# One pair of resident B tiles instead of four rotating ones in a selective scan on one core

## The chip, the cores and the metric

The kernel runs on one core of one Trainium2 chip, as one program without collectives. The metric is the device time of one execution in microseconds (us), the median of several executions. All data is float32.

## The reference

Input is an image of 2 x 48 x 48 positions with 768 channels. Two layers follow each other, `x = x + layer(_gn(x))` for both, where `_gn` is a group normalization. The first is neighbourhood attention: 12 heads of 64, each position attends to a 7 x 7 window. The second is a bidirectional Mamba block, and it takes nearly all the time. For each image its 2304 positions are a sequence, and 1536 inner channels carry 16 states each. In one direction, the part that the change touches computes:

```python
def _selective_scan(u, delta, A, Bm, Cm):
    def step(h, inp):
        d_t, B_t, C_t, u_t = inp
        dA = jnp.exp(d_t[..., None] * A)
        h = dA * h + (d_t * u_t)[..., None] * B_t[:, None, :]
        y = jnp.einsum('bdn,bn->bd', h, C_t)
        return (h, y)
...
x_dbl = jnp.einsum('bdl,ed->bel', x, x_proj_w)
dt = x_dbl[:, :dt_rank]
Bm = x_dbl[:, dt_rank:dt_rank + n]
Cm = x_dbl[:, dt_rank + n:]
delta = jax.nn.softplus(jnp.einsum('brl,dr->bdl', dt, dt_proj_w) + dt_proj_b[None, :, None])
y = _selective_scan(x, delta, A, Bm, Cm) + x * Dp[None, :, None]
```

So the state of (channel, state number) is a first-order recurrence along the sequence. Its factor is exp(delta * A), its input is delta * u * B, and B and C depend on position and state number but not on channel. The second direction runs over the reversed sequence with weights of its own.

## The kernel before

**Tiling.** Channels lie on the 128 partitions, in ND = 12 tiles; the sequence runs along the free axis in NCH = 6 chunks of CL = 384 positions. A pass is one image (b) and one direction (back), and `passes` lists the 24 chunks in their order: image 0 forward, image 0 backward, image 1 forward, image 1 backward. One unit is one chunk and one channel tile k, so there are 288 units, 12 per chunk. The 16 states of a unit are worked in NSG = 4 groups of SG = 4.

**One group (`group` in `scan`).** A tile `hb` of four rows of 386 cells holds four states side by side, each with a spare cell ahead of and behind its 384 positions.

- L1231, ScalarE (ACT): copies eight numbers from `state`, or zeros in the first chunk of a pass, into the spare cells (columns 0 and 385) of the four rows of the B tile `bc[g]`. These are the states that enter the chunk, with a cell that restarts the recurrence at a row's end. The copy is made per unit, because each channel tile has its own states while the B values are the same for all twelve.
- L1225, VectorE (DVE) or GpSimd (POOL): the fill. It multiplies delta*u (in PSUM as `du` for DVE, in SBUF as `u` for POOL) by `bc[g]` into `hb`. It reads all 386 columns, so it needs both the load and the copy.
- L1247, ACT: one exponential per state, into one of the two PSUM tiles `da0` and `da1`, which hold two states each.
- L1258, DVE: one scan instruction for two states. It frees that `da` tile, so ACT can be two scans ahead at most.
- L1273, POOL: the product with C, from `bc[NSG + g]`. L1281, ACT: keeps the leaving states in `state`. L1290, TensorE (PE): transposes and sums the four states into `py`.

**The tiles of B and C.** For each chunk `chunk` takes eight new tiles with tags bc0 to bc7, one buffer per tag, and SyncE (SP) loads each with one broadcast from `xdf` or `xdb` (L1381, 768 KB): bc0 to bc3 are B with 386 columns, of which the load writes columns 1 to 384; bc4 to bc7 are C. A load waits until the last fill of the chunk before (unit k = 11) has read its tile.

**What sets the order.** `add` only lists a piece of work with its engine, an estimated duration and a key (a due time in units). What it reads and writes is given in buffers and numbered parts of them. `Order.run` plans all of it ahead: per engine it picks a work whose predecessors are done, EARLY work with a bonus of 20 units, and an order over all engines comes out. The instructions are then issued in that order, each engine runs its own in order, and the tile framework adds the semaphores for what it finds overlapping in memory. In the plan a load occupies SP for 400 ns and its data is there some 2.1 us plus its transfer later. In the plan of before, the first copy of a chunk (k = 0) depends on the load, since the load is listed as writing all parts of `bc[g]`, the ends (part 1) among them.

Attention of image 0 runs ahead of the scan phase and uses the same tags for other tiles: `FIRST` names them for `oT`, q and v, and `HEAD` for the first chunk's projections. Attention of image 1 and the projections run beside the scans, as jobs in the gaps.

Of the kernel before, what the change touches and what calls it, by code (L numbers as in the profile page):

```python
# [10 lines left out]
F32 = mybir.dt.float32  # L11
# [82 lines left out]
class Order:  # L94
# [15 lines left out]
    @staticmethod  # L110
    def cells(uses):
        for x in uses:
            buf, parts = x if isinstance(x, tuple) else (x, range(x.parts))
            for p in (parts,) if isinstance(parts, int) else parts:
                yield buf, p
# [130 lines left out]
def tile_kernel(  # L246
# [30 lines left out]
        Buf(f"da{i}", parts=2, ap=psum.tile([P, 1024], F32, tag=f"da{i}", name=f"da{i}"))  # L277
        for i in range(2)
    ]
    zero = res.tile([P, SG, 2], F32, tag="zero", name="zero")  # L280
    nc.gpsimd.memset(zero, 0.0)
    one = res.tile([P, KB, 2], F32, tag="one", name="one")
    nc.gpsimd.memset(one, 1.0)
# [35 lines left out]
    def sb(tag, shape, n, parts=1):  # L319
        return Buf(f"{tag}_{n}", wk, shape, tag, BUFS.get(tag, 1), parts)  # L320
# [8 lines left out]
    def add(eng, ns, fn, key, r=(), w=(), job=False, size=0, after=None, early=0, alt=None, due=False, opens=None):  # L329

        news = [x[0] if isinstance(x, tuple) else x for x in w]

        def issue():
            for v in news:
                if v.ap is None:
                    v.ap = v.pool.tile(v.shape, F32, tag=v.tag, name=v.name, bufs=v.bufs)
            fn()

        if eng == "PE":

            ns *= 1.04 if key < 0 else 1.05
        return order.add(eng, ns, issue, key, r, w, job, size, after, early, alt, due, opens)
# [837 lines left out]
    def scan(ch, k, x, dlj, duj, vt):  # L1180
# [30 lines left out]
        def group(g):  # L1211
            m = f"{n}_{g}"
            now = at + 0.25 * g
            hb = sb("hb", [P, SG * W], m, SG + 1)
            body = (hb, range(SG))
            kept = lambda o: state[:, k, 2 * SG * g + o : 2 * SG * (g + 1) + o].rearrange(
                "p (j e) -> p j e", e=2
            )
            was = zero if ch["first"] else kept(0) if back else kept(1)

            def first():
                by, on = (dus[:, ju, :], nc.gpsimd) if filled.eng == "POOL" else (du[:, :W], nc.vector)
                on.tensor_mul(  # L1225
                    cells(hb, SG), by.unsqueeze(1).to_broadcast([P, SG, W]), bc[g].ap
                )

            if k == 0 or not ch["first"]:
                add(  # L1230
                    "ACT", 98, lambda: nc.scalar.copy(bc[g][:, :, ends], was), now - 0.4,  # L1231
                    [(state, k * NSG + g)], [(bc[g], 1)], early=EARLY,
                )
            on = {"DVE": dve(SG * W), "POOL": SG * W * 2.03 + 15}
            main, other = ("DVE", "POOL") if g in (0, 1) else ("POOL", "DVE")
            filled = add(
                main, on[main], first, now - (0.35 if main == "POOL" else 0.1),
                [du, duj, bc[g]], [hb], after=marks.get(marks["n"] - 6),
                alt=(other, on[other]) if g in (1, 2, 3) else None,
            )  # L1240

            def step(j):
                i = g * SG + j
                da = das[j // 2 % 2]
                add(
                    "ACT", act(cl, 1) + 45,
                    lambda: nc.scalar.activation(  # L1247
                        cells(da, 2)[:, j % 2, h], dl[:, jd, c], AF.Exp, scale=q["A"][:, k, i : i + 1]
                    ),
                    now + 0.06 * j - 0.06, [dlj], [(da, j % 2)], due=True,  # L1250
                )

            def two_steps(j):
                da = das[j // 2 % 2]
                at2 = (slice(None), slice(j * W, (j + 2) * W))
                mark = add(
                    "DVE", (4 * W + 42) / 0.96,
                    lambda: nc.vector.tensor_tensor_scan(  # L1258
                        flip(hb[at2]), flip(da[:, : 2 * W]), flip(hb[at2]), 0.0, ALU.mult, ALU.add
                    ),  # L1260
                    now + 0.06 * j, [da], [(hb, (j, j + 1, SG))],
                )
                marks[marks["n"]] = mark
                marks["n"] += 1

            for j in range(0, SG, 2):
                step(j)
                step(j + 1)
                two_steps(j)

            add(
                "POOL", SG * cl * 2.03 + 10,
                lambda: nc.gpsimd.tensor_mul(  # L1273
                    cells(hb, SG)[:, :, h], cells(hb, SG)[:, :, h], bc[NSG + g][:, :, c]
                ),
                now + 0.25, [body, bc[NSG + g]], [body],
            )
            if not ch["final"]:
                add(
                    "ACT", 90,  # L1280
                    lambda: nc.scalar.copy(  # L1281
                        kept(0)[:, :, 1:2], cells(hb, SG)[:, :, leaves : leaves + 1]
                    ),
                    now + 0.3, [body, (hb, SG)], [(state, k * NSG + g)],
                )

            def add_up():
                for j in range(SG):
                    for t in range(nt):
                        nc.tensor.matmul(  # L1290
                            py[:tp, t * P : (t + 1) * P], cells(hb, SG)[:, j, h][:, tb[t]], ident,
                            start=False,
                            stop=g == NSG - 1 and j == SG - 1 and t == nt - 1,
                            is_transpose=True, skip_group_check=True,
                        )

            add(
                "PE", SG * nt * 109 + 60, add_up, now + 0.45, [body, py], [py], early=FIRM,
                opens=False if g == NSG - 1 else None,
            )  # L1300
# [62 lines left out]
    def chunk(b, back, i, at):  # L1363

        l0, cl = CHUNKS[i]
        s = f"{b}_{back}_{i}"
        dt = sb("dt", [RK + 1, CL], s)
        src = xd[back][b]
        add(
            "SP", 400, lambda: nc.sync.dma_start(dt[:, :cl], src[: RK + 1, l0 : l0 + cl]), at - 1.4,  # L1370
            [(src, cols(l0, cl))], [dt], size=RK * cl * 4,
        )
        bc = []
        for g in (0, 1, 2, NSG, 3, NSG + 1, NSG + 2, NSG + 3):

            o = int(g < NSG)
            t = sb(f"bc{g}", [P, SG, CL + 2 * o], s, 1 + o)
            r = RK + 1 + g * SG
            add(
                "SP", 400,  # L1380
                lambda t=t, r=r, o=o: nc.sync.dma_start(  # L1381
                    t[:, :, o : o + cl], src[r : r + SG, l0 : l0 + cl].partition_broadcast(P)
                ),
                at - 1 + 0.25 * (g % NSG) + 0.3 * (g >= NSG), [(src, cols(l0, cl))], [t],
                size=P * SG * cl * 4,
            )
            bc.append((g, t))
        bc = [t for g, t in sorted(bc, key=lambda x: x[0])]
        ends = (0, NCH - 1)

        ys = ()
        if (b, back, i) == passes[-1]:
            parts = [sb(tag, [P, n, CL], f"y{tag}{n}", n) for tag, n in (("uz", 2 * KB), ("uz", KB), ("u", KB))]
            ys = [(y, k) for y in parts for k in range(y.parts)]
        return dict(
            q=par[back], b=b, back=back, l0=l0, cl=cl, dt=dt, bc=bc, s=s, i=i, ys=ys,
            first=i == ends[back], final=i == ends[not back],
        )


    passes = [
# [4 lines left out]
    ]  # L1406

    FIRST = {
        "xn": ("xc", "uz"), "oT": ("bc0", "bc1", "bc2", "bc3"), "halves": 2, "k": ("hb",), "q": ("bc4", "bc5"),
        "v": ("bc6", "bc7"), "s": 0, "pt": 1, "po": ("py", "du"), "vw": ("u", "dlt"),  # L1410
        "ev": ("ev", "vt"),
    }
# [3 lines left out]
    }  # L1416
    LATE = 4
    FIRM = 4.0
    HEAD = ("bc4", "bc5", "bc6", "bc7", "bc0", "bc1")
    A0, A1, P1 = (-56, -16), (50, 118), 118  # L1420
    norms, norms0, stats = [], [], []
    for b in range(nb):
# [37 lines left out]
    for p, (b, back, i) in enumerate(passes):  # L1460
        ch = None
        for k in range(ND):
            units.append((p, b, back, i, k))
    chunks = {}

    deltas = {}

# [8 lines left out]
    for x, (p, b, back, i, k) in enumerate(units):  # L1476
        if x % KB == 0 and x + KB < len(units):
            ahead(x + KB)
        scan(chunks[p], k, x, *deltas.pop(x))
        if x == len(units) - 1:  # L1480
            ch = chunks[p]
            last_out_proj(b, ch["l0"], ch["cl"], ch["ys"], x - 1, x + 3)
        elif back and k == ND - 1:
            for h, (l0, cl) in enumerate(PIECES[i]):
                at = x + 2.5 + 5 * h if b else 188 + 2 * (2 * (NCH - 1 - i) + h)
                out_proj(b, l0, cl, at, at + (4.5 if b else 1.8))
# [55 lines left out]
```

## Time and profile before

| what | value |
|---|---|
| median of 3 runs | 7038.78 us (7036.31 to 7051.21) |
| span of the profiled execution | 7054.5 us |
| profiled execution's own time | not given apart from its span |
| DVE busy, 1060 to 7020 us | 5631.57 of 5960 us |
| POOL busy, same stretch | 5436.23 us |
| PE busy, same stretch | 5333.59 us |
| ACT busy, same stretch | 4654.78 us |
| scans (L1258) | 2304 of 1746 ns |
| fills (L1225) | 657 on DVE of 1743 ns, 495 on POOL of 3203 ns |
| products with C (L1273) | 1152 of 3186 ns |
| exponentials (L1247) | 4608 of 584 ns |
| copies of entering states (L1231) | 960 of 197 ns, and 16 of zeros |
| broadcast loads (L1381) | 192 of 768 KB |

The first 1036 us are attention of image 0 and projections; the scan phase fills the rest. A line number such as L1231 is that of the kernel before. The busy times are per engine; idle time matters only where the engine bounds the end. "[0.73 <-DMA bc<-xdb]" behind an instruction says that its engine stood idle for 0.73 us before it and that the last thing to come was that transfer. SPq is SyncE's queue of transfers: its rows show the issue and not the transfer's end.

### The profile page before, as it was taken

How to read it: one execution, taken by the hardware profiler on the slowest of the kernel's cores; microseconds unless marked ns; L12 is line 12 of the kernel's file. 1: busy time of each engine (PE TensorE's matmuls, PEld its weight loads, DVE VectorE, ACT ScalarE, POOL GpSimd, SP SyncE). 2: the span in 40 equal slices, each digit the busy share in tenths (PEclk: the TensorE clock that was granted, in tenths of full speed). 3: DMA queues.
4: the chain of work that ended last, by engine and by line, in shares of the span. 5: the costliest groups of instructions: out<-in, count | busy, mean ns of one | idle time of the engine just before them, and what ended most of it. 6: DMA issues, size and time to landing. Idle time of an engine off the chain costs nothing.

```text
span 7054.5 us, 105645 instructions
## 1 busy us (share of the span) xinstructions
PE 6334.5 (90%) x38151; PEld 4844.6 (69%) x38151; DVE 6061.2 (86%) x6217; ACT 4970.2 (70%) x10948; POOL 5447.5 (77%) x1951
## 2 busy tenths in 40 slices
PE   7999989999989998999988888888888898999888
PEld 5666656666667776676666656666678887777777
DVE  2354449999999999998898999999999999999998
ACT  1333248788887788887888778788876667777765
POOL 0000008888989999988898878999999999999997
PEclk9999989999999999999999999999999999999999
DMA  6565454444556444555444354343466676655553
GB/s 190 172 200 172 139 161 131 134 144 151 157 160 191 151 149 141 152 170 150 126 144 131 113 166 127 107 143 108 140 179 191 174 220 199 191 177 158 162 169 105
DMA packets 1337698, 1101.32 MB, mean 156 GB/s; under 512 B 136328, under 2 KB 1327416, under 8 KB 1337144
## 3 DMA queue, kind: packets, MB, share of 16 engines
q1 hardware_dynamic: 1337176, 1094.56, 52.1%
q8 instruction: 303, 4.96, 0.3%
q14 instruction: 219, 1.79, 0.1%
HBM read 881.41 MB, written 213.57 MB: 155 GB/s over the span
## 4 chain that ended last, share of the span: by engine, by line
DVE 39%; PE 19%; ACT 14%; POOL 12%; issue 9%; DMA 6%; SPq 1%; DVEq 0%; POOLq 0%; ACTq 0%
DVE hb L1258 25%; POOL hb L1273 8%; DVE hb L1225 7%; ACT da L1247 4%; PE mm_qk L382 4%; DVE uz_u L935 4%; POOL hb L1225 3%; PE py L1290 2%; PE mm_ao L382 2%; PE mm_v L382 2%; PE mm_xin L382 2%; ACT uz_u L928 1%; PE da L825 1%; ACT pr L785 1%; ACT L1163 1%
## 5 line engine op out<-in xcount | busy, mean ns | idle before, releaser
L1258 DVE TENSOR_TENSOR_SCAN hb<-da,hb 128x772 f32<-128x772 f32 x2304 | 3924.9, 1746 | 187.3 <-ACT da L1247 155.1
L1273 POOL TENSOR_TENSOR hb<-hb,bc 128x1536 f32<-128x1536 f32 x1152 | 3653.7, 3186 | 381.0 <-DVE hb L1258 338.3
L1247 ACT ACTIVATE da<-dlt,A 128x384 f32<-128x384 f32 x4608 | 2677.2, 584 | 915.2 <-DVE hb L1258 845.8
L1290 PE MATMUL py<-ident,hb 128*128 128x128 f32 x13824 | 1754.3, 279 | 264.3 <-POOL hb L1273 255.2
L1290 PEld LDWEIGHTS py<-ident,hb 128*128 128x128 f32 x13824 | 1570.9, 143 | 523.5 <-POOL hb L1273 413.6
L1225 POOL TENSOR_TENSOR hb<-u,bc 128x1544 f32<-128x1544 f32 x495 | 1584.6, 3203 | 22.6 <-PE py L1290 14.9
L1225 DVE TENSOR_TENSOR hb<-du,bc 128x1544 f32<-128x1544 f32 x657 | 1141.4, 1743 | 34.3 <-ACT du L1202 24.8
L1175 POOL TENSOR_TENSOR u<-dlt,u 128x384 f32<-128x384 f32 x288 | 263.8, 918 | 532.7 <-DMA bc<-xdf 412.6
L382 PE MATMUL mm_xin<-xc,w_x 128*128 128x390 f32 x1656 | 593.3, 504 | 25.3 <-DVE uz_u L935 16.2
L382 PE MATMUL mm_z<-xc,w_z 128*128 128x384 f32 x1728 | 608.1, 492 | 7.8 <-ACT dlt L1157 4.9
L382 PE MATMUL mm_out<-stage_y,w_o 128*128 128x192 f32 x3168 | 560.7, 332 | 18.1 <-ACT dlt L1157 6.4
L1491 PE MATMUL py<-ident 128*128 128x128 f32 x4431 | 550.4, 277 | 0.0
L382 PEld LDWEIGHTS mm_out<-stage_y,w_o 128*128 128x128 f32 x3168 | 522.0, 194 | 29.3 <-ACT dlt L1157 10.6
L1491 PEld LDWEIGHTS py<-ident 128*128 128x128 f32 x4431 | 503.3, 143 | 28.9 <-issue 26.0
L901 POOL MEMSET xc<- 128x18 f32 x4 | 0.5, 116 | 637.2 <-DVE sm L779 637.2
L382 PEld LDWEIGHTS mm_xin<-xc,w_x 128*128 128x128 f32 x1656 | 311.3, 195 | 238.3 <-issue 36.7
L935 DVE SCALAR_TENSOR_TENSOR uz_u<-mm_xin,conv_w,uz_u 128x384 f32<-128x384 f32 x792 | 428.3, 607 | 52.0 <-ACT uz_u L928 49.4
L382 PE MATMUL mm_qk<-xc_xn,w_qk 128*128 128x384 f32 x1296 | 459.1, 500 | 14.7 <-DMA w_qk<-in_w_qkv 3.1
L382 PEld LDWEIGHTS mm_z<-xc,w_z 128*128 128x128 f32 x1728 | 314.3, 192 | 194.4 <-issue 8.9
L382 PEld LDWEIGHTS mm_qk<-xc_xn,w_qk 128*128 128x128 f32 x1296 | 240.2, 194 | 173.8 <-issue 19.5
L785 ACT ACTIVATE pr<-pr,sm 128x308 f32<-128x308 f32 x432 | 234.5, 544 | 127.5 <-DVE sm L779 127.2
L1306 PE MATMUL py<-ident,vt 128*128 128x128 f32 x864 | 156.3, 292 | 146.3 <-ACT yt L1316 145.9
(163 smaller groups left out, 6780.9 us busy)
## 6 DMA issues: line engine op xcount, KB each, us to landing
w_o<-in_w_opT SPq DMA_DIRECT2D x264, 384.0 KB
bc<-xdf SPq DMA_DIRECT2D x96, 768.0 KB
bc<-xdb SPq DMA_DIRECT2D x96, 768.0 KB
w_qk<-in_w_qkv SPq DMA_DIRECT2D x144, 384.0 KB
w_x<-in_w_inT SPq DMA_DIRECT2D x144, 384.0 KB
w_z<-in_w_inT SPq DMA_DIRECT2D x144, 384.0 KB
w_ao<-in_w_out SPq DMA_DIRECT2D x72, 384.0 KB
u<-uf SPq DMA_DIRECT2D x48, 576.0 KB
```

Source lines behind the costliest of these rows:

```text
L382: nc.tensor.matmul(acc[:m, o0 : o0 + cl], wb[:, wi, wo : wo + m], xb[:, xi, xo : xo + cl], start=c == 0, stop=c == n - 1,)
L785: nc.scalar.activation(pr[j].ap, pr[j].ap, AF.Exp, bias=sm[:, j : j + 1], scale=-1.0, accum_out=sm[:, 2 + j : 3 + j],)
L825: nc.tensor.transpose(bank(pt, 512 - P)[:nk, k * P : (k + 1) * P], pr[j][:, c0 : c0 + nk], ident,)
L935: nc.vector.scalar_tensor_tensor(u, px[:, at[j] : at[j] + cl], q["conv_w"][:, k, j : j + 1], u, ALU.mult, ALU.add,)
L1175: lambda j=j: nc.gpsimd.tensor_mul(u[:, j, h], dl[:, j, c], u[:, j, h]), at + 0.06 + 0.25 * j,
L1225: on.tensor_mul(cells(hb, SG), by.unsqueeze(1).to_broadcast([P, SG, W]), bc[g].ap)
L1247: lambda: nc.scalar.activation(cells(da, 2)[:, j % 2, h], dl[:, jd, c], AF.Exp, scale=q["A"][:, k, i : i + 1]),
L1258: lambda: nc.vector.tensor_tensor_scan(flip(hb[at2]), flip(da[:, : 2 * W]), flip(hb[at2]), 0.0, ALU.mult, ALU.add),
L1273: lambda: nc.gpsimd.tensor_mul(cells(hb, SG)[:, :, h], cells(hb, SG)[:, :, h], bc[NSG + g][:, :, c]),
L1290: nc.tensor.matmul(py[:tp, t * P : (t + 1) * P], cells(hb, SG)[:, j, h][:, tb[t]], ident, start=False, stop=g == NSG - 1 and j == SG - 1 a ...
L1306: nc.tensor.matmul(py[:tp, t * P : (t + 1) * P], vt[:, tb[t]], ident, start=t == 0, stop=False, is_transpose=True, skip_group_check=True,)
L1491: nc.tensor.matmul(marks["py"][:, CL : CL + P], ident, ident, start=False, stop=False, is_transpose=True, skip_group_check=True,)
```

## The change

B's four tiles become two tiles `pairs` of eight states (tags bc0 and bc2, [128, 8, 386] each). They are taken once, when the scan phase begins, and kept to its end. Each has three parts in the planner's book: 0 and 1 are the two halves of four rows, 2 is the spare cells of all eight rows. The loads stay as they are in number, size and key, but each now lists only its half as written, and they are listed when the chunk's first unit is (`broadcasts`), no longer three units ahead. The copy of entering states is made once for two groups: 16 numbers in place of two times eight, with a planned 110 ns in place of 98, listed when the even group is. It reads the states of both groups, writes part 2, and lists the chunk's columns of `xdf` or `xdb` as read. The fill of a group reads its half and part 2. C's tiles stay. `FIRST` and `HEAD` follow: `oT` takes one tile of six channel pairs from bc0 or bc2 where it took two of three, and the last `HEAD` tile is bc2 where it was bc1.

```diff
-            was = zero if ch["first"] else kept(0) if back else kept(1)
+            pair, half = bc[g // 2], g % 2
...
-                    cells(hb, SG), by.unsqueeze(1).to_broadcast([P, SG, W]), bc[g].ap
+                    cells(hb, SG), by.unsqueeze(1).to_broadcast([P, SG, W]),
+                    pair[:, half * SG : (half + 1) * SG, :],
...
-            if k == 0 or not ch["first"]:
+            if half == 0 and (k == 0 or not ch["first"]):
+                was = zero if ch["first"] else kept(0 if back else 1, 2)
                 add(
-                    "ACT", 98, lambda: nc.scalar.copy(bc[g][:, :, ends], was), now - 0.4,
-                    [(state, k * NSG + g)], [(bc[g], 1)], early=EARLY,
+                    "ACT", 110, lambda: nc.scalar.copy(pair[:, :, ends], was), now - 0.4,
+                    [(state, k * NSG + g), (state, k * NSG + g + 1), (xd[back][b], cols(l0, cl))], [(pair, 2)], early=EARLY,
                 )
...
-                [du, duj, bc[g]], [hb], after=marks.get(marks["n"] - 6),
+                [du, duj, (pair, half), (pair, 2)], [hb], after=marks.get(marks["n"] - 6),
...
-        bc = []
-        for g in (0, 1, 2, NSG, 3, NSG + 1, NSG + 2, NSG + 3):
-
-            o = int(g < NSG)
-            t = sb(f"bc{g}", [P, SG, CL + 2 * o], s, 1 + o)
...
+    def broadcasts(ch, at):
+
+        src, l0, cl, s = xd[ch["back"]][ch["b"]], ch["l0"], ch["cl"], ch["s"]
+        if not pairs:
+            pairs.extend(
+                sb(f"bc{2 * p}", [P, 2 * SG, CL + 2], "pair", 3) for p in range(NSG // 2)
+            )
+        bc = []
+        for g in (0, 1, 2, NSG, 3, NSG + 1, NSG + 2, NSG + 3):
+
+            r = RK + 1 + g * SG
+            if g < NSG:
+                t, part, wide = pairs[g // 2], g % 2, slice(1, cl + 1)
+                of = slice(part * SG, (part + 1) * SG)
+                w = (t, part)
+            else:
+                t, of, wide = sb(f"bc{g}", [P, SG, CL], s), slice(0, SG), slice(0, cl)
+                bc.append(t)
+                w = t
+            add(
+                "SP", 400,
+                lambda t=t, r=r, of=of, wide=wide: nc.sync.dma_start(
+                    t[:, of, wide], src[r : r + SG, l0 : l0 + cl].partition_broadcast(P)
+                ),
+                at - 1 + 0.25 * (g % NSG) + 0.3 * (g >= NSG), [(src, cols(l0, cl))], [w],
+                size=P * SG * cl * 4,
+            )
+        ch["bc"] = pairs + bc
...
-        "xn": ("xc", "uz"), "oT": ("bc0", "bc1", "bc2", "bc3"), "halves": 2, "k": ("hb",), "q": ("bc4", "bc5"),
+        "xn": ("xc", "uz"), "oT": ("bc0", "bc2"), "halves": 1, "k": ("hb",), "q": ("bc4", "bc5"),
...
-    HEAD = ("bc4", "bc5", "bc6", "bc7", "bc0", "bc1")
+    HEAD = ("bc4", "bc5", "bc6", "bc7", "bc0", "bc2")
...
             ahead(x + KB)
+        if k == 0:
+            broadcasts(chunks[p], x)
         scan(chunks[p], k, x, *deltas.pop(x))
```

More of the change, by code (lines that the diff above doesn't have):

```diff
@@ L279, in tile_kernel @@
     ]
-    zero = res.tile([P, SG, 2], F32, tag="zero", name="zero")
+    zero = res.tile([P, 2 * SG, 2], F32, tag="zero", name="zero")
     nc.gpsimd.memset(zero, 0.0)
@@ L1215, in group @@
             body = (hb, range(SG))
-            kept = lambda o: state[:, k, 2 * SG * g + o : 2 * SG * (g + 1) + o].rearrange(
+            kept = lambda o, n=1: state[:, k, 2 * SG * g + o : 2 * SG * (g + n) + o].rearrange(
                 "p (j e) -> p j e", e=2
             )
-            was = zero if ch["first"] else kept(0) if back else kept(1)
+            pair, half = bc[g // 2], g % 2
             def first():
@@ L1273, in group @@
                 lambda: nc.gpsimd.tensor_mul(
-                    cells(hb, SG)[:, :, h], cells(hb, SG)[:, :, h], bc[NSG + g][:, :, c]
+                    cells(hb, SG)[:, :, h], cells(hb, SG)[:, :, h], bc[2 + g][:, :, c]
                 ),
-                now + 0.25, [body, bc[NSG + g]], [body],
+                now + 0.25, [body, bc[2 + g]], [body],
             )
@@ L1372, in chunk @@
         )
-        bc = []
-        for g in (0, 1, 2, NSG, 3, NSG + 1, NSG + 2, NSG + 3):
-            o = int(g < NSG)
-            t = sb(f"bc{g}", [P, SG, CL + 2 * o], s, 1 + o)
[L1378 to L1388, printed above, removed]
         ends = (0, NCH - 1)
@@ L1395, in chunk @@
         return dict(
-            q=par[back], b=b, back=back, l0=l0, cl=cl, dt=dt, bc=bc, s=s, i=i, ys=ys,
+            q=par[back], b=b, back=back, l0=l0, cl=cl, dt=dt, s=s, i=i, ys=ys,
             first=i == ends[back], final=i == ends[not back],
         )
+    def broadcasts(ch, at):
[24 more added lines that the diff above has]
+        ch["bc"] = pairs + bc
     passes = [
@@ L1463, in tile_kernel @@
             units.append((p, b, back, i, k))
-    chunks = {}
+    chunks, pairs = {}, []
     deltas = {}
```

## The prediction

> **What bounds the kernel now.** I read the busy time of each engine first, then the groups of instructions, then who waited for whom on ACT and DVE between 1060 and 7020 us, and last the order of time around one change of chunk.
>
> ```profile
> span 7054.5 us, 105645 instructions
> 1060.00:7020.00 5960.00, 5333.59 (x32999) 4186.83 (x32998) 5631.57 (x4701) 4654.78 (x10100) 5436.23 (x1936) 0.98 0.52 154
> ```
>
> The second line is the scan phase: PE 5334, its weight loads 4187, DVE 5632, ACT 4655, POOL 5436 us of 5960. DVE works 94% of the phase and sets its length; POOL, which takes the C products and 495 of the fills, is close behind with 91%. ACT has 1305 us idle, so making ACT's work shorter pays only where DVE waits for ACT.
>
> ```profile
> L1258 DVE TENSOR_TENSOR_SCAN hb<-da,hb 128x772 f32<-128x772 f32 x2304 | 3924.9, 1746 | 187.3 <-ACT da L1247 155.1
> L1231 ACT COPY bc<-state 128x8 f32<-128x8 f32 x960 | 182.9, 197 | 126.6 <-DVE hb L1225 64.6 <-POOL hb L1225 29.7 <-DMA bc<-xdb 15.1
> ACT da L1247 <- DVE hb L1258: 845.8, 1242, 3.8
> ACT bc L1231 <- DVE hb L1225: 64.6, 129, 4.1
> ACT bc L1231 <- POOL hb L1225: 29.7, 48, 1.6
> ACT bc L1231 <- DMA bc<-xdb: 16.6, 13, 3.3
> ACT bc L1231 <- DMA bc<-xdf: 12.8, 12, 2.4
> DVE uz_u L935 <- ACT uz_u L928: 37.6, 36, 3.9
> DVE hb L1225 <- ACT du L1202: 16.3, 22, 1.7
> ```
>
> The reader is to see three things. ACT waits 845.8 us for scans to free a `da` tile: as a rule it is two scans ahead and no more. DVE waits 155.1 + 37.6 + 16.3 = 209 us for ACT, of 328 us idle in all. And the copy of entering states has waited for a broadcast load 25 times, 29.4 us in all. The copy writes columns 0 and 385, the load columns 1 to 384: no number is in both, and still the copy does not start before the load is done. One change of chunk shows it, on SP's queue, ACT and DVE:
>
> ```profile
> 3578.71 0.40 SPq L1381 DMA_DIRECT2D bc<-xdb  x1
> 3585.03 0.38 SPq L1381 DMA_DIRECT2D bc<-xdb  x1
> ```
> ```profile
> 3585.72 0.20 ACT L1231 COPY bc<-state 128x8 f32<-128x8 f32 x1 [0.73 <-DMA bc<-xdb]
> 3585.82 0.58 ACT L1247 ACTIVATE da<-dlt,A 128x384 f32<-128x384 f32 x1
> 3593.01 0.20 ACT L1231 COPY bc<-state 128x8 f32<-128x8 f32 x1 [1.43 <-DMA bc<-xdb]
> ```
> ```profile
> 3576.90 1.74 DVE L1225 TENSOR_TENSOR hb<-du,bc 128x1544 f32<-128x1544 f32 x1
> 3583.21 1.76 DVE L1225 TENSOR_TENSOR hb<-du,bc 128x1544 f32<-128x1544 f32 x1
> 3587.82 1.76 DVE L1258 TENSOR_TENSOR_SCAN hb<-da,hb 128x772 f32<-128x772 f32 x1 [1.03 <-ACT da L1247]
> ```
>
> These are g = 0 and g = 1. The last fill of the old chunk ends at 3578.64, its load goes out at 3578.71, and the new chunk's copy starts at 3585.72, after 7.0 us. For g = 1: fill ends 3584.97, load 3585.03, copy 3593.01, after 8.0 us. ACT stood 0.73 us for the first, and DVE 1.03 us for ACT. So I read that the framework takes all between the first and the last cell of the copy as touched, and puts a semaphore between copy and load, whichever is issued first.
>
> **What the skill says.** "DMA: Bandwidth & Descriptors", section "Anatomy of one DMA — SWDGE (gpsimd) path": the semaphore moves only when the last byte has landed, some 2.0 us beside the bytes at 436 GB/s. For 786,432 bytes that would be an estimated 3.8 us (the page's path is another than SP's); the trace has 7.0 and 8.0 us with the queues half busy, and I use the trace. "Perfetto Trace Analysis", section "DMA Instruction — HWDGE (DVE, Sync)": the data movement lies outside the slice shown; the trace agrees, with 0.40 us rows. "ScalarE: Activation LUTs", section "What ACT_TABLE_LOAD costs": an instruction without pointer operands takes 186 ns + 0.833 ns per element, and neighbours overlap by some 93 ns. For 8 elements 193 ns; the trace has 197. For 16 I take 204 ns.
>
> **The change part by part.**
>
> *Fewer copies.* 976 become 488. One costs ACT 197 ns less the overlap of 93, so 0.10 us: 49 us less. The copies' waits for fills (94.3 us) halve, as one copy waits only for the later fill of two: 47 us less. ACT gains 96 us of 5960. Of that DVE sees at least nothing, at most all 96 (it waits 209 for ACT). I take a fifth, as ACT waits for DVE far more often than the reverse: **-19 us**.
>
> *The coarser wait inside a chunk.* A copy now needs both fills of the unit before, and both fills of the next unit need it. Over the 11 steps of each chunk, from the end of the later of two fills to the start of the earlier of the next two the trace has 7.4 us or more in 95 of 100 cases, median 13. The two other fills of the unit lie between and hide it: 0. Were that cover gone, each of some 500 copies would cost up to half a microsecond.
>
> *The wait at a change of chunk.* This is the dear part. In the plan of before the copy of k = 0 stands behind its own load's estimated landing, so ACT meets it late: 29.4 us of waiting in all. In the change the load lists its half alone and the copy part 2 alone, so the plan sees no tie and puts the EARLY copy right behind the last fill of both groups. The load of the second half is ready at that very moment too. SP, mostly idle, takes it at once; ACT takes the copy when its instruction in hand ends. ACT is busy 78%, and SP sometimes; I take 0.65 for "load first". There are 23 changes of chunk with two copies: 46, so 30 copies stand behind both loads and 16 behind the first alone (or neither).
>
> Behind both: the load takes 7.5 us, the copy's turn comes 0.5 us after the fill (the median lag in the trace is 0.45), so ACT stands 7.0 us, and everything queued on it, the exponentials first. A copy and two exponentials add 1.2 before a scan can start: 8.2. DVE has the rest of a scan and one more (0.9 + 1.7), and work that needs no exponentials: (5632 - 3925)/5960 = 29% of 8.2, so 2.3. Loss 8.2 - 4.9 = 3.3 us, times 30 = **+99**. Bounds: 2 us with full cover, 5 with none but half a scan, and 21 to 37 cases.
>
> Behind the first alone: the two last fills lie 5.0 us apart (median), so the first load still lacks 2.0 us; 3.2 with the restart, under 4.9. A quarter lie under 2.6 us apart: 16 x 0.3 = **+5**.
>
> Late loads: in 7 of the 46 the second load is issued over 4 us after its fill, 7.0 on average, as SP stands in another wait. The copy then waits that long too: 7 x 0.65 x 7.0 = **+32**, 0 to 60.
>
> *Old waits that go.* The 29.4 us of ACT; of the two shown DVE felt one. Half: **-15**.
>
> *SP.* Where the copy comes first, the second load waits on SP's queue for it, a few us, and the transfers behind it too; the new chunk's first fills come 14 us after the old ones' end (median), so mostly 0. Listing the loads later keeps their keys. `FIRST` and `HEAD` concern the start: the norm ahead of `HEAD` needs all of attention, so bc2 is free by then: 0.
>
> *Recovery.* DVE's 119 us of idle that ACT doesn't cause can take back some: a tenth of 136, **-13**.
>
> Sum: 99 + 5 + 32 - 19 - 15 - 13 = +89. The profiled span 7054.5 would become 7144; it lies 15.7 us above the median of the runs, and no time beside the span is given, so I carry the difference to the median: 7038.8 + 89 = **7128 us**.
>
> **The rivals.** *Faster*: copy and load don't touch for the framework, or the copies are planned ahead of both loads (then loads wait, with 14 us of room). Then only ACT's 96 us count, a third of them and the old waits: -32 - 15, about 7000 (6985 to 7020). For it speaks that ACT's copies wait on fills 177 times; against it that the copy waited for loads that write other cells. It decides by the place of the copy among the loads in ACT's order. *No change*: ACT's stalls fall mostly where DVE has fills and jobs in hand, loss under 1.5 us each, and the relief pays it back: about 7040. The copy at 3593.01 speaks for it: it stood 1.43 us and DVE did not stop. *Worse*: late loads grow more frequent, since loads now wait for copies and copies for loads, in turn, on two in-order queues; 5 us for 35 copies plus 60: +220 less 40, about 7220.
>
> **How the numbers follow.** Forecast 0.56 (7060 to 7180), worse 0.20 (7180 to 7270), no change 0.11, faster 0.13. What this kernel's measurement can tell is about 0.2%, 14 us. The range 7030 to 7220 leaves out most of "faster" and half of "worse". Slower by over 0.2%: 0.76; within: 0.11; faster: 0.13.
>
> **What would show it.** In the changed trace, copies of 16 numbers, 488 of some 204 ns; ACT's idle before them with a B load as releaser, from 29 us to between 150 and 300 over up to 46 cases, 6 to 8 us where long; DVE's wait for `da` from 155 us to some 250 or more; scans, fills and products as long as before. Wrong if the copies' waits for loads stay under 50 us, or if they are long and DVE's idle does not grow.

## The result, and the profile after

The changed kernel takes 7254.64 us (median of 4 runs, 7246.0 to 7266.82), the one before 7037.55 us in the same comparison: 217 us more, a ratio of 1.0299 with a 95% interval of 1.0281 to 1.0318. The profiled span is 7257.1 us, against 7054.5. The direction and the mechanism were as forecast; the size was not: 89 us had been forecast, and the time lies above the range.

The scan phase on the same columns as before (PE, its weight loads, DVE, ACT, POOL, clock, DMA share, GB/s), from the page and from the busy times of one stretch:

```profile
span 7257.1 us, 105492 instructions
```
```profile
1060.00:7220.00 6160.00, 5392.23 (x33067) 4250.05 (x33066) 5618.14 (x4684) 4602.42 (x9612) 5462.41 (x1944) 0.96 0.48 149
```

DVE's work is the same within 14 us, ACT's is 52 us less, and DVE's idle grew from 328 to 542 us. So nothing became slower in itself; DVE waits more. The groups of instructions and the list of waits say for whom:

```profile
L1260 DVE TENSOR_TENSOR_SCAN hb<-da,hb 128x772 f32<-128x772 f32 x2304 | 3928.6, 1750 | 317.5 <-ACT da L1249 284.9 <-POOL hb L1225 8.0 <-POOL hb L1275 3.4
L1233 ACT COPY bc_pair<-state 128x16 f32<-128x16 f32 x480 | 99.9, 209 | 237.9 <-DMA bc_pair<-xdb 117.3 <-DMA bc_pair<-xdf 64.6 <-DVE hb L1225 24.4
```
```profile
ACT bc_pair L1233 <- DMA bc_pair<-xdb: 154.1, 21, 13.4
ACT bc_pair L1233 <- DMA bc_pair<-xdf: 80.2, 16, 9.8
ACT bc_pair L1233 <- DVE hb L1225: 24.4, 43, 2.9
ACT bc_pair L1233 <- POOL hb L1225: 16.2, 20, 2.0
```

The copies are 488 with the zeros, 209 ns each, and ACT stands in them 234.3 us for B loads, in 37 cases and up to 13.4 us, where it stood 29.4 us before. The copies' waits for fills fell from 94.3 to 40.6 us. DVE's wait for `da` rose from 155.1 to 284.9 us. Three more of DVE's waits for ACT grew with it, from 37.6, 16.3 and 8.6 us:

```profile
DVE uz_u L935 <- ACT uz_u L928: 53.0, 37, 8.8
DVE hb L1225 <- ACT du L1202: 32.8, 27, 4.2
DVE sm L800 <- ACT pr L785: 23.0, 12, 9.7
```

In all, DVE's waits for ACT rose from 217 to 395 us, which is 178 of the 214 us that it idles more; its waits for PE rose from 69 to 97 us. The granted PE clock of the profiled execution fell from 0.975 to 0.960. It is no rival cause: in e5 below, where ACT alone is held up, it is 0.950, and DVE's waits for PE grow alike, to 95 us.

The same change of chunk as in the prediction, in time, on SP's queue, ACT and DVE:

```profile
3657.03 0.73 SPq L1408 DMA_DIRECT2D bc_pair<-xdb  x1
3662.11 1.52 SPq L1408 DMA_DIRECT2D bc_pair<-xdb  x2
```
```profile
3661.57 1.20 ACT L1249 ACTIVATE da<-dlt,A 128x384 f32<-128x384 f32 x2 [1.50 <-DVE hb L1260]
3669.41 0.21 ACT L1233 COPY bc_pair<-state 128x16 f32<-128x16 f32 x1 [6.63 <-DMA bc_pair<-xdb]
3669.61 2.31 ACT L1249 ACTIVATE da<-dlt,A 128x384 f32<-128x384 f32 x4
```
```profile
3661.46 1.74 DVE L1225 TENSOR_TENSOR hb<-du,bc_pair 128x1544 f32<-128x1544 f32 x1
3663.11 0.55 DVE L705 TENSOR_TENSOR xr_x<-mm_ao,xr_x 128x384 f32<-128x384 f32 x1
3664.17 3.40 DVE L1260 TENSOR_TENSOR_SCAN hb<-da,hb 128x772 f32<-128x772 f32 x2
3670.84 3.42 DVE L1260 TENSOR_TENSOR_SCAN hb<-da,hb 128x772 f32<-128x772 f32 x2 [2.22 <-ACT da L1249]
```

The old chunk's other fill of the pair ends at 3662.1 on POOL; the second load goes out at 3662.11; the copy is next in ACT's queue and starts at 3669.41, when that load is done. Behind it four exponentials have piled up. DVE works off two scans and two small jobs of attention (one of their instructions is the row at 3663.11) and then stands, too: for 2.22 us here.

### The profile page after: what moved, and what is told of

It is laid out like the page before. It is cut to its first block, busy times and chain, and to the rows that moved or that the text cites. A ratio compares the mean times of both kernels' runs of the same rounds, so it can differ in the third digit from the quotient of the medians.

```text
span 7257.1 us, 105492 instructions
## 1 busy us (share of the span) xinstructions
PE 6400.8 (88%) x38260; PEld 4914.9 (68%) x38260; DVE 6052.3 (83%) x6207; ACT 4918.2 (68%) x10460; POOL 5479.4 (76%) x1961
## 5 line engine op out<-in xcount | busy, mean ns | idle before, releaser
L1260 DVE TENSOR_TENSOR_SCAN hb<-da,hb 128x772 f32<-128x772 f32 x2304 | 3928.6, 1750 | 317.5 <-ACT da L1249 284.9
L1292 PE MATMUL py<-ident,hb 128*128 128x128 f32 x13824 | 1782.8, 282 | 312.8 <-POOL hb L1275 301.8
L1292 PEld LDWEIGHTS py<-ident,hb 128*128 128x128 f32 x13824 | 1600.4, 145 | 560.4 <-POOL hb L1275 436.0
L1225 POOL TENSOR_TENSOR hb<-u,bc_pair 128x1544 f32<-128x1544 f32 x505 | 1615.3, 3201 | 50.2 <-PE py L1292 43.8
L1225 DVE TENSOR_TENSOR hb<-du,bc_pair 128x1544 f32<-128x1544 f32 x647 | 1126.4, 1746 | 70.8 <-ACT du L1202 41.0
L1509 PE MATMUL py<-ident 128*128 128x128 f32 x4540 | 572.3, 279 | 0.0
L1509 PEld LDWEIGHTS py<-ident 128*128 128x128 f32 x4540 | 524.9, 144 | 31.9 <-issue 29.0
```

The source lines that it names most:

```text
L1225: on.tensor_mul(cells(hb, SG), by.unsqueeze(1).to_broadcast([P, SG, W]), pair[:, half * SG : (half + 1) * SG, :],)
L1260: lambda: nc.vector.tensor_tensor_scan(flip(hb[at2]), flip(da[:, : 2 * W]), flip(hb[at2]), 0.0, ALU.mult, ALU.add),
L1292: nc.tensor.matmul(py[:tp, t * P : (t + 1) * P], cells(hb, SG)[:, j, h][:, tb[t]], ident, start=False, stop=g == NSG - 1 and j == SG - 1 a ...
L1509: nc.tensor.matmul(marks["py"][:, CL : CL + P], ident, ident, start=False, stop=False, is_transpose=True, skip_group_check=True,)
```

## The experiments

Each was compared with the kernel before on the same chip; "before" ran at 7045 to 7048 us there.

**e1: the planner knows of the wait.** The only edit to the changed kernel:

```diff
-                    [..., (xd[back][b], cols(l0, cl))], [(pair, 2)], early=EARLY,
+                    [..., (xd[back][b], cols(l0, cl)), (pair, (0, 1))], [(pair, 2)], early=EARLY,
```

> The changed kernel, except that the planner is told that the copy of sixteen needs both loads of its pair, so that it is ordered behind their estimated landing. Nothing else is touched: resident pairs, one copy for two groups. Theory A (ACT stands in the copies that were ordered blind right behind the loads, and that is all of the loss): ACT's idle for B loads falls from 234 us to under 60, the time to 7010 to 7070 us. Rival B (the pair itself costs: the copy tied to two groups, the loads' halves in one tile): idle falls as well, but the time stays above 7150.

Measured: 7085.93 us, ratio 1.0052 (1.0036 to 1.0069). ACT's idle for B loads is 16.8 us in all, DVE's wait for `da` 153.8, as before the change:

```profile
L1260 DVE TENSOR_TENSOR_SCAN hb<-da,hb 128x772 f32<-128x772 f32 x2304 | 3924.2, 1746 | 189.9 <-ACT da L1249 153.8 <-POOL hb L1225 15.2 <-DVE hb L1225 1.4
ACT bc_pair L1233 <- DMA bc_pair<-xdb: 8.9, 8, 2.1
ACT bc_pair L1233 <- DMA bc_pair<-xdf: 7.9, 6, 2.3
```

The loss against the kernel before is 40 us in place of 217: 177 us go with the blind order (the copies planned without sight of the loads), and 40 stay. The time is 16 us over the range that theory A gave, and far from B's 7150.

**e2: half of it.** As e1 with `(pair, (0, 1) if g == 0 else ())`.

> As e1, but only the copies of the first pair (groups 0 and 1) are ordered behind their loads; those of the second pair stay blind. In the changed kernel ACT's idle ahead of the first copies of a chunk is 114 us at the first pair and 148 us at the second. Theory A: the loss goes with that idle, 217 x 114/262 = 94 us come back, 7160 us (7120 to 7190). Rival B: within 30 us of the changed kernel or of e1, with no such share.

Measured: 7203.3 us, ratio 1.0222 (1.0207 to 1.0238). ACT still stands 147.9 us for B loads, 86 us less than in the changed kernel. The loss is 158 us, so 59 us came back, not 94, and the time lies above A's range. The direction is A's, the share is smaller. The shares that were expected, 114 and 148 us, do not come out of the trace of the changed kernel, which has 99 and 147 us of idle at the first copies of the two pairs. In e2 that is 49 us at the first pair, which ordering behind the estimated landing empties by half only, and 117 us at the second, which was left blind.

**e3: the blind order without the pair.** Four tiles and single copies as before, with two lines of the change:

```diff
-                at - 1 + 0.25 * (g % NSG) + 0.3 * (g >= NSG), [(src, cols(l0, cl))], [t],
+                at - 1 + 0.25 * (g % NSG) + 0.3 * (g >= NSG), [(src, cols(l0, cl))], [(t, 0)],
...
-                    [(state, k * NSG + g)], [(bc[g], 1)], early=EARLY,
+                    [(state, k * NSG + g), (xd[back][b], cols(l0, cl))], [(bc[g], 1)], early=EARLY,
```

> The kernel before with its four tiles per chunk and one copy per group, and one thing of the change: a load is listed as writing columns 1 to 384 alone and the copy lists xdf or xdb as read, so the planner sees no tie between load and copy. Theory A: now 92 first copies can stand behind their loads; at six in ten and 7 us each some 385 us of ACT idle, at the change's rate of 217/262 a loss of 320, about 7350 us (7200 to 7450). Rival B (the pair makes the loss): no pair here, 7030 to 7060 us.

Measured: 7306.24 us, ratio 1.0368 (1.0353 to 1.0384). ACT stands 251.3 us for B loads (41 cases), DVE waits 349.5 us for `da`:

```profile
L1231 ACT COPY bc<-state 128x8 f32<-128x8 f32 x960 | 182.4, 197 | 361.0 <-DMA bc<-xdf 123.1 <-DMA bc<-xdb 114.4 <-DVE hb L1225 74.7
```

With no pair at all the loss is 261 us. The order alone makes such a loss, and rival B falls as the main cause. The idle is less than the 385 us expected; that copies which follow one another closely share a stop is my reading and was not counted.

**e4: copy first.** The changed kernel, with both loads of a pair listed after the copy of k = 0 and waiting for it (`after=entered`), so that the semaphore between them works the other way round.

```diff
-                add(
+                entered = add(
                     "ACT", 110, lambda: nc.scalar.copy(pair[:, :, ends], was), now - 0.4,
...
+                if k == 0:
+                    for load in ch["loads"][g // 2]:
+                        load(entered)
```

> The changed kernel with the order turned round: both loads of a pair are listed after the copy of the chunk's first unit and wait for it, so the copy waits for fills alone. Loads go out some 5 us later for the first half; the new chunk's first fills come 14 us after the last old ones, so mostly hidden. Theory A: ACT's idle for B loads under 10 us, time 7010 to 7070 us. Rival B: above 7150. If loads are now late instead, DVE and POOL wait for B loads in the fills (L1225), which they do not so far.

Measured: 7059.08 us, ratio 1.002 (1.0012 to 1.0027). ACT's idle for B loads is gone from its waits; fills wait 12.4 us for the later loads:

```profile
L1225 POOL TENSOR_TENSOR hb<-u,bc_pair 128x1544 f32<-128x1544 f32 x501 | 1603.5, 3203 | 30.7 <-PE py L1295 25.1 <-DMA bc_pair<-xdb 4.2 <-DMA bc_pair<-xdf 1.3
L1225 DVE TENSOR_TENSOR hb<-du,bc_pair 128x1544 f32<-128x1544 f32 x651 | 1131.5, 1744 | 54.9 <-ACT du L1202 37.9 <-DMA bc_pair<-xdb 6.9 <-PE py L1295 4.4
```

So all but 14 of the 217 us go with ACT's stops. What was left was the size: why did a stop of 7.3 us (the mean of the copies behind both loads) cost nearly 7 us, when I had 3.3? Rival C says that my price of a stop is right and the loads do something more.

**e5 and e6: ACT held up by itself.** The kernel before, in its own order to the last instruction, with

```diff
+                def entering():
+                    if k == 0 and g % 2 == 0:
+                        for _ in range(16):
+                            nc.scalar.copy(state.ap, state.ap)
+                    nc.scalar.copy(bc[g][:, :, ends], was)
```

and 8 in place of 16 in e6.

> The kernel before in its own order, with ACT held up by itself: ahead of the first copies of groups 0 and 2 of every chunk (48 places) ACT copies the state tile onto itself 16 times, some 0.42 us each, 6.8 us in a row. No load, no pair and no other order is touched; the planner does not know of it. Theory A (a standing ACT takes the scans with it nearly at once, so the term mis-sized was the cover): 5 to 6 us lost per place, 7280 to 7330 us. Rival C (my cover of 4.9 us was right and the change's loss has a second source): 3.3 us per place, about 7200 us.

> As e5 with 8 copies in a row, 3.4 us. Theory A with a cover of about 3 us and a restart of 1.2: 1.5 to 2.5 us per place, 7110 to 7160 us. Rival C (cover 4.9): 0, 7035 to 7060 us. If the loss is in proportion to the hold without any cover, 3 us per place, 7180 us.

Measured: e5 7437.41 us, ratio 1.055 (1.0536 to 1.0565); e6 7223.61 us, 1.0249 (1.0235 to 1.0264). The copies did not overlap as I had reckoned. Two rows of ACT's order of time and the groups of e5:

```profile
3746.38 8.81 ACT L1233 COPY state<-state 128x396 f32<-128x396 f32 x16
3773.95 8.81 ACT L1233 COPY state<-state 128x396 f32<-128x396 f32 x16
```
```profile
L1264 DVE TENSOR_TENSOR_SCAN hb<-da,hb 128x772 f32<-128x772 f32 x2304 | 3928.1, 1747 | 505.1 <-ACT da L1253 471.7 <-POOL hb L1225 13.1 <-ACT du L1202 0.5
L1233 ACT COPY state<-state 128x396 f32<-128x396 f32 x768 | 400.5, 521 | 22.8
```

The scans of e6:

```profile
L1264 DVE TENSOR_TENSOR_SCAN hb<-da,hb 128x772 f32<-128x772 f32 x2304 | 3927.1, 1747 | 326.1 <-ACT da L1253 292.8 <-POOL hb L1225 13.9
```

A hold is 8.81 us in e5 and 4.39 us in e6. Per place (48) the time grew by 389/48 = 8.1 and 175/48 = 3.65 us. That is the hold less 0.7 us, twice. Both times lie above every range that was given, in part because the holds were longer than the 6.8 and 3.4 us reckoned with. Of the 389 us of e5, 362 are DVE's waits for ACT. Neither a load nor a pair was touched, so rival C falls: a standing ACT alone costs that much.

**e10 and e11: a short hold, and one in mid-chunk.** As e6 with 2 copies, and with `k == 6` in place of `k == 0`.

> As e5 and e6 with 2 copies in a row, 1.0 us at each of 48 places, 49 us in all. If a standing ACT costs its whole length however short it is (e5: 389 for 393 us, e6: 175 for 193): +40 to +50 us, 7090. If there is a cover of about 3 us that is free: within 10 us of before.

> As e6, but the 8 copies in a row come at the chunk's seventh channel tile (k = 6; 40 places, as the first chunk of a pass has no copies there), 4.0 us each, 161 us in all. If ACT has no free cover anywhere: +145 us, 7190. If the change of chunk is the tight place, where loads and the softplus fall together: under +80.

Measured: e10 7071.87 us, ratio 1.0033 (1.002 to 1.0046); holds of 1.06 us, 0.5 us lost at each. e11 7174.39 us, ratio 1.0178 (1.0165 to 1.0192); holds of 4.39 us at 40 places, 128/40 = 3.2 us lost at each. So even 1 us is half paid, and mid-chunk a stop costs nearly what it does at the change: my cover of 4.9 us is nowhere.

**e7 and e9: more copies, fewer copies.** The kernel before with each copy twice, and with 440 of 976 copies not issued (those of odd groups with k from 1 to 11). The edit of e9:

```diff
-                    "ACT", 98, lambda: nc.scalar.copy(bc[g][:, :, ends], was), now - 0.4,
+                    "ACT", 98,
+                    lambda: k > 0 and g % 2 or nc.scalar.copy(bc[g][:, :, ends], was), now - 0.4,
```

> The kernel before with each of its 976 copies of entering states made twice in a row, unknown to the planner: 0.10 us more of ACT each, 98 us in all, twice what the change saves, in the other direction. If the fifth that I let DVE see holds: +20 us, 7058. If the relief is worth nothing: within 8 us of before. If all of it reaches DVE: +98.

> The kernel before in its own order, and 440 of its 976 copies of entering states are not issued: those of the odd groups for k of 1 to 11, so half of the states restart from what the chunk's first channel tile left there. The planner doesn't know of it. This is the change's relief of ACT alone, without pair, loads or a new order. My step said a fifth of the time: -19 us. If ACT's time counts as it did where copies were doubled (+84 us for 976): -38 us, about 7008. If time saved is not worth what time added costs, since an order planned ahead has to wait for other engines anyway: within 10 us of before.

Measured: e7 7132.45 us, ratio 1.0111 (1.0093 to 1.013); ACT's busy time grew by 179 us, since the second copy of the same cells does not overlap the first (two in a row take 0.44 us, one takes 0.20). e9 7040.62 us, ratio 0.9995 (0.9989 to 1.0002): no difference, though ACT is busy 44 us less and its copies wait 28 us less. DVE's wait for `da` stays as it was:

```profile
L1259 DVE TENSOR_TENSOR_SCAN hb<-da,hb 128x772 f32<-128x772 f32 x2304 | 3924.3, 1746 | 185.1 <-ACT da L1248 151.0 <-POOL hb L1225 14.1 <-ACT du L1202 0.5
```

The 179 us added to ACT cost half of themselves; the 44 us taken from it, in an unchanged order, brought nothing that can be measured.

**e8: copy first, four tiles.** The order of e4 in the kernel before.

> The kernel before, four tiles per chunk and one copy per group, with the order of e4: a tile's load is listed after the chunk's first copy into it and waits for it. It takes away the 29.4 us that ACT waits for loads, and tells e4's remaining 0.2% apart: if the pair (one copy tied to two groups) costs that, this runs at 7015 to 7040 us; if the later loads do, at 7050 to 7070 as e4.

Measured: 7045.21 us, ratio 0.9999 (0.999 to 1.0008), though ACT's 29.4 us of waiting for loads are down to about 0.7. This lies between the two ranges: the later loads cost nothing that can be measured, and the old waits, gone, brought nothing either. Against this e4, which differs by the pair, its 488 fewer copies and the order planned with them, is 14 us slower. So the pair brings no time even in the best order tried.

**e12: later copies.** e8 without `early=EARLY` for the copies.

> e8 without the bonus of EARLY for the copies of entering states, so they are planned where ACT has nothing more urgent, not right behind the fill. In e8 ACT still stands 98 us in these copies for fills. If such standing counts in full: 7045 less 50 or more, 6990. If it falls where ACT would wait for scans anyway: 7030 to 7055.

Measured: 7087.01 us, ratio 1.0046 (1.0032 to 1.006). The copies' waits for fills stay at 101.9 us (102.3 in e8), so the standing that the change was to remove is still there. The idea failed; where the 41 us more are lost stays open.

## Why the prediction was wrong

**Right: the mechanism.** A copy is ordered right behind the last fill, beside a load with which it shares no number, and waits for it. e3 makes the loss without the pair; with the pair, e1 takes away 177 us of it and e4 all but 14. **Right: the counts.** Of 46 copies I put 30 behind both loads and 16 behind the first; in the trace, by what each copy waits for, they are 28 and 18. ACT's idle for B loads was to be 150 to 300 us and is 234; in the 28 it is 7.3 us on average, against 7.0.

**Wrong, and the step that failed: the cover of 4.9 us in "Loss 8.2 - 4.9 = 3.3 us".** The loss is near 6.6: the stop less the 0.7 us that e5 and e6 leave uncharged. I let DVE live for 4.9 us on a running scan, one more, and 2.3 us of work that needs no exponentials. The changed trace has 32 stops of more than 3 us, 7.26 us on average. Over such a stop and the 1.2 us behind it DVE had 2.3 us of scans and only 0.9 us of other work, and stood 5.2. Much of the "other" work needs ACT too, as the three lines of DVE's waits above show.

And the cover that there is was not free. e5 and e6 run the order of before, so each scan can be set beside the same scan of before. The holds come in twos, 2 to 9 scans apart, one at each pair of groups; the next two come some 90 scans later. The table takes the second hold of each two, 23 places, so that no other hold falls in between. It has the delay of a scan against its like in before, less the delay just ahead of the hold, as a mean in us:

| scan after the hold begins | 1st | 2nd | 3rd | 11th | 33rd | 81st |
|---|---|---|---|---|---|---|
| e6, hold of 4.39 us | 2.0 | 3.4 | 3.7 | 4.0 | 3.9 | 3.7 |
| e5, hold of 8.81 us | 4.5 | 8.0 | 8.3 | 8.7 | 8.5 | 8.6 |

The first scan is half covered, as I had reasoned. By the third scan nearly all is paid, and nothing to speak of comes back before the next hold. When a hold begins, ACT has begun exponentials for only 0.8 of a scan ahead. My reading, argued and not shown by a run of its own: the lead is what hides ACT's own long pieces, such as a softplus of 3.7 us with its table loads, so a stop has little of it to use.

In the terms of the prediction: the 28 copies behind both loads cost 28 x (7.3 - 0.7) = 185 us, where 99 were forecast. The 18 behind the first load alone stand 42 us, some 33 at the same price, where 5 were forecast. The old 25 stops give 29.4 - 17.5 = 12 us back at that price, where 15 were forecast, though e8 shows no gain from it. 14 us stay in e4. The sum is 220, and 217 were measured.

**Wrong: "Fewer copies", -19.** e9 has 72 of the 96 us of that relief and gains nothing that can be measured. **Wrong: "Late loads", +32.** Of the 28 second loads behind which a copy stood, only one was issued over 4 us late; the loads themselves took 7.0 us from issue to copy at the first pair and 8.0 us at the second. That this term is about as much too high as the copies behind the first load were too low is luck. **Wrong: "Recovery", -13.** The table shows none. **Right: the coarser wait inside a chunk** cost little: 40.6 us of waits for fills in place of 94.3. **Right: SP, `FIRST` and `HEAD`**: the first scan starts at 1053.8 us, at 1056.7 before.

The rival "worse" gave about 7220 us for a reason that did not hold (late loads and more cases); its terms, 35 x 5 + 60, make 235 and not 220. Its time was nearer than mine, not its cause.

What stays open: the price fits the changed kernel better than its variants. Counted over the stops that the lists of waits put down to B loads, with the same 14 and 12 us, it gives 210 us for the changed kernel, 9 for e1 and 132 for e2, and for e3, which has no pair and so no 14 us, 211; measured are 217, 40, 158 and 261. So each of the three variants costs some 25 to 50 us more by something that was not tried apart. In e1 the fills wait 18.2 us for the copies, which now come behind both landings; in the changed kernel that was 6.4 on POOL. In the profiled execution of e1, 34 us are lost in the last three chunks of image 0. The 14 us of e4 show late: its scans are 20 us ahead of before at the first chunk of image 1's backward pass and level with it one chunk later, and in between DVE stands 10.9 us almost in a row for the output projection. Behind the last scan come 43.2 us, in place of 36.7. e8 keeps 15 us of its lead there, and its end is as in before. Why the planned order of e4 differs at these places is open.

## What to carry to other kernels

Where a planner orders the work and something else adds the semaphores, a dependency that the semaphores enforce but the plan lacks is dear: the plan puts the two pieces side by side, and the later one holds its whole queue for a transfer's length. Price a stop of a feeding engine at nearly its full length before you grant it a cover, even if that engine is idle a fifth of the time: here 4.39 and 8.81 us of hold cost 3.65 and 8.1. And a saving on such an engine is not the mirror of a cost: doubling a small piece cost 84 us, leaving out nearly half of it gained none.

## What the runs showed of the hardware

Sixteen copies of 396 numbers from a tile onto itself took 8.81 us on ACT, 0.55 us each, where unrelated neighbours in the same queue overlap (a copy of 0.18 us is followed after 0.09). And a copy of 16 numbers takes 209 ns against 197 for 8.
